# A written order for the Outlook stage: all engines, one mix a step, bands sorted by pairs of heads

## The chip, the cores and the metric

The kernel runs on one core of one Trainium2 chip. The metric is the device time of one execution in microseconds (us); of several executions the median is given. TensorE (PE) multiplies matrices, VectorE (DVE) and ScalarE (ACT) work element by element, GpSimd (POOL) and SyncE (SP) mostly issue transfers (DMAs) here. Each engine takes its own list of instructions in order and waits on semaphores of the others. Tiles lie in the on-chip memory with 128 partitions; TensorE's products land in a second small memory, PSUM.

## The reference

Two layers on an image batch of 4 x 32 x 32 positions with 384 channels. Layer 0 is an attention with group masks, followed by a mixture of four experts, two of them per token. Layer 1 is an Outlook attention, followed by a feed-forward net whose weights are Kronecker products. All is float32. The change touches the Outlook attention and its borders:

```python
v = einsum('bhwc,oc->bhwo', x, Wv)                      # x: normalised input of the layer
patches = the 3 x 3 neighbourhood of v at every position   # b, n, 9, heads, d
a = einsum('bhwc,oc->bhwo', x, Wa).reshape(b, n, 12, 9, 9)
attn = softmax(a * d ** -0.5, axis=-1)
out = einsum('bnhpq,bnqhd->bnphd', attn, patches)       # 9 outputs per position
y = sum of the 9 outputs at the positions they belong to   # a scatter-add over the 3 x 3 window
x = x + einsum('bhwc,oc->bhwo', y, Wo)
t = x + gelu(norm(x) @ kron(c_fc_1, c_fc_2).T) @ kron(c_proj_1, c_proj_2).T
```

A position gathers from its 3 x 3 window and scatters to its 3 x 3 window, so an output position depends on the values of a 5 x 5 window, with 25 coefficients per head.

## The kernel before

The 4096 tokens are 32 tiles of 128 tokens (4 rows of an image), 8 tiles an image. `attention` and `experts` come first; `rest` (L2246) then loads the residual x, the weights of Outlook, and calls `outlook` (L1764) and `Kron.run` (L2106). The Outlook stage works tile by tile:

- `scores` (L1852): normalises tile i on DVE (`xn`, L147), transposes it on PE (`ps_tr`, L155) and copies it on ACT (`xnT`, L156). PE multiplies it by Wa in two halves of 486 columns (`ps_a`, L1862); DVE takes maxima (L1871) and subtracts them (L1872), ACT takes exp (L1877), DVE sums, inverts and scales (L1879 to L1886, here called the share). Four DMAs on SyncE's queue shift the parts of the shares that belong one row up or down into the tiles `up` and `down` of this tile and its neighbours (L1898 to L1903); they copy from on-chip memory to on-chip memory. PE also makes the values `ps_v` (L1906), which ACT copies to `v` (L1910).
- `band` (L1912), two tiles later: ACT copies the outer rows of `u` (L1919, L1920), DVE adds the inner ones (L1921 to L1923), PE shifts within a row by three products (`ps_c`, L1927), DVE masks the borders (`co`, L1935). The result goes to a room in DRAM (L1942) in such a layout that reading it back with another row length (L1948) gives the band matrix of the tile: 128 source tokens by 260 target positions by 12 heads, heads innermost. Reading back waits for the writing; a band is 1560 KB.
- `gather` (L1953), three tiles after `band`: for each head PE multiplies the values (32 columns) by the band of that head (`ps_y`, L1964). Four heads go to the four groups of 32 columns of PE. The moving operand is `bands[b, t][:, j : j + hi - lo, h]`, one float out of twelve. An image is worked in two halves of 512 target positions. The last gather of a half is followed by three copies on ACT (`y`, L1973).
- `mix` (L1976): PE multiplies `y` by Wo for one tile (`ps_wo`, L1980), DVE adds the product to x (L1984). The four tiles of a half are mixed in the two steps after its last gather, two a step.

The residual of the last 15 tiles is not complete when the stage begins: `add(i)` (L1831) gathers two expert outputs per token by indirect DMAs on POOL's queue (L1540) into two buffers, adds them on DVE (L1835) and measures mean and variance (L137, L138). At the end of an image, `net.scale` takes the square root on ACT and the reciprocal on DVE (L143, L144). `loads` (L2272) issues the loads of later images at steps 1, 2 and 5 and those of Kron at step 8 (L2062 to L2080; each has a few sums on DVE, L2072 to L2077). From step 25 on `kron.begin` and `kron.shrink` (L2083, L2091) prepare the feed-forward net of the first 16 tiles: begin takes 16 pairs of statistics (L128, L129) at once.

The order of work: a step scores tile `step`, then adds, then runs what is due.

```python
at(o + 2, band, b, t)
at(o + 2 + LAG, gathered, b, 0 if t < 5 else 1, t)
...
with tc.manual_schedule(engines={eng.SP, eng.Pool}):
    outlook(net, wv, wa, wo, range(done, NT), router, kron, loads)
```

SyncE and POOL keep this written order; the order of PE, DVE and ACT in this stage is chosen by a scheduler when the program is built, which may take an instruction ahead of others and break a group of products in two. PSUM tiles for transposes, values and mixes come from one pool of two (`ps_m`).

Of the kernel before, what the change touches and what calls it, by code (L numbers as in the profile page):

```python
# [10 lines left out]
FP = mybir.dt.float32  # L11
BF = mybir.dt.bfloat16
AF = mybir.ActivationFunctionType
# [4 lines left out]
P = 128  # L18
# [1745 lines left out]
def outlook(net, wv, wa, wo, left, router, kron, loads):  # L1764
# [15 lines left out]
    with ExitStack() as ctx:  # L1780
# [5 lines left out]
        bp = ctx.enter_context(tc.tile_pool(name="ol_band", bufs=5, reuse_waits="tile"))  # L1786
# [42 lines left out]
        left = list(left)  # L1829

        def add(i):  # L1831
            for n in range(2):
                y = bp.tile([P, C], FP, name="yt", tag="yt", bufs=2)
                router.gather(y, i, n)
                nc.vector.scalar_tensor_tensor(  # L1835
                    net.x(i), y, router.weight[n][:, i : i + 1], net.x(i), ALU.mult, ALU.add
                )
            net.measure(work, i, net.x(i))

        attn, vs, bands, ys, moved = {}, {}, {}, {}, {}  # L1840
# [11 lines left out]
        def scores(b, t):  # L1852

            i = b * NB + t
            xn = work.tile([P, C], FP, name="xn", tag="xn")
            net.ln_apply(xn, i, i, net.mv, net.rs)
            xnT = work.tile([P, KC, P], FP, name="xnT", tag="xnT")
            net.transposed(ps_m, "m", xn, xnT, nc.scalar.copy)
            pa = ps_a.tile([P, 2, 512], FP, name="ps_a", tag="a")
            for hh in range(2):  # L1860
                for k in range(KC):
                    nc.tensor.matmul(  # L1862
                        pa[:, hh, :HW_], lhsT=xnT[:, k, :], rhs=wa[:, k, hh * HW_ : (hh + 1) * HW_],
                        start=k == 0, stop=k == KC - 1,
                    )

            a = ap_.tile([P, 3, 2, 3, PW], FP, name="attn", tag="attn")
            for hh in range(2):
                mx = work.tile([P, PW], FP, name="a_max", tag="a_max")
                given = pa[:, hh, :HW_].rearrange("p (q e) -> p q e", q=K2)  # L1870
                nc.vector.tensor_reduce(mx, given.rearrange("p q e -> p e q"), AX.X, ALU.max)  # L1871
                nc.vector.tensor_tensor(  # L1872
                    a[:, :, hh, :, :], given.rearrange("p (y x) e -> p y x e", y=3),
                    mx.unsqueeze(1).unsqueeze(1).to_broadcast([P, 3, 3, PW]), ALU.subtract,
                )
            flat = a.rearrange("p y s x e -> p (y s x e)")
            nc.scalar.activation(flat, flat, AF.Exp, scale=QK_SCALE)  # L1877
            rows = work.tile([P, 2, 3, PW], FP, name="a_rows", tag="a_rows", bufs=1)
            nc.vector.tensor_tensor(rows, a[:, 0], a[:, 1], ALU.add)  # L1879
            nc.vector.tensor_tensor(rows, rows, a[:, 2], ALU.add)  # L1880
            sm = work.tile([P, 2, PW], FP, name="a_sum", tag="a_sum")
            nc.vector.tensor_tensor(sm, rows[:, :, 0, :], rows[:, :, 1, :], ALU.add)
            nc.vector.tensor_tensor(sm, sm, rows[:, :, 2, :], ALU.add)
            nc.vector.reciprocal(sm, sm)
            for qi in (0, 2, 1):
                nc.vector.tensor_tensor(  # L1886
                    a[:, qi], a[:, qi], sm.unsqueeze(2).to_broadcast([P, 2, 3, PW]), ALU.mult
                )
            attn[b, t] = a


            flat = [a[:, qi].rearrange("p s x e -> p (s x e)") for qi in range(3)]
            if t == 0:
                moved[b, 0] = room(b, 0)
            if t + 1 < NB:
                moved[b, t + 1] = room(b, t + 1)
            down, up = moved[b, t]
            nc.sync.dma_start(out=up[: P - IMG, :], in_=flat[0][IMG:, :])  # L1898
            nc.sync.dma_start(out=down[IMG:, :], in_=flat[2][: P - IMG, :])
            if t:  # L1900
                nc.sync.dma_start(out=moved[b, t - 1][1][P - IMG :, :], in_=flat[0][:IMG, :])
            if t + 1 < NB:
                nc.sync.dma_start(out=moved[b, t + 1][0][:IMG, :], in_=flat[2][P - IMG :, :])  # L1903
            ps = ps_m.tile([P, 512], FP, name="ps_v", tag="m")
            for k in range(KC):
                nc.tensor.matmul(  # L1906
                    ps[:, :C], lhsT=xnT[:, k, :], rhs=wv[:, k, :], start=k == 0, stop=k == KC - 1
                )
            v = vs[b, t] = vp.tile([P, C], FP, name="v", tag="v")
            nc.scalar.copy(v, ps[:, :C])  # L1910

        def band(b, t):  # L1912


            H3 = 3 * H6
            u = work.tile([P, 6, 5, H3], FP, name="u", tag="u")
            down, up = (m.rearrange("p (g y e) -> p g y e", g=6, y=3) for m in moved.pop((b, t)))
            own = attn.pop((b, t))[:, 1].rearrange("p s x (y e) -> p (s x) y e", y=3)
            nc.scalar.copy(u[:, :, 0, :], down[:, :, 0, :])  # L1919
            nc.scalar.copy(u[:, :, 4, :], up[:, :, 2, :])  # L1920
            nc.vector.tensor_tensor(u[:, :, 1:3, :], down[:, :, 1:3, :], own[:, :, 0:2, :], ALU.add)  # L1921
            nc.vector.tensor_tensor(u[:, :, 3, :], own[:, :, 2, :], up[:, :, 1, :], ALU.add)
            nc.vector.tensor_tensor(u[:, :, 2, :], u[:, :, 2, :], up[:, :, 0, :], ALU.add)  # L1923
            pc = ps_c.tile([P, 512], FP, name="ps_c", tag="c")
# [22 lines left out]
            m = bands[b, t] = bp.tile([P, BAND, NH], FP, name="band", tag="band")  # L1947
# [5 lines left out]
        def gather(b, half, t):  # L1953

            first, last = (0, 4) if half == 0 else (3, 7)
# [3 lines left out]
            for c in range(KC):  # L1959
                if t == first:  # L1960
                    ys[c] = ps_y.tile([P, 512], FP, name=f"ps_y{c}", tag=f"y{c}")
                for n in range(4):
                    h = 4 * c + n
                    nc.tensor.matmul(  # L1964
                        ys[c][32 * n : 32 * n + 32, lo - 512 * half : hi - 512 * half],
                        lhsT=vs[b, t][:, h * HD : (h + 1) * HD],
                        rhs=bands[b, t][:, j : j + hi - lo, h],
                        start=t == first, stop=t == last, skip_group_check=True,
                    )
            if t == last:  # L1970
                y = work.tile([P, KC, 512], FP, name="y", tag="y", bufs=1)
                for c in range(KC):
                    nc.scalar.copy(y[:, c, :], ys[c])  # L1973
                return y

        def mix(b, half, n, y):  # L1976
            i = b * NB + 4 * half + n
            ps = ps_m.tile([P, 512], FP, name="ps_wo", tag="m")
            for k in range(KC):
# [3 lines left out]
                )  # L1983
            nc.vector.tensor_tensor(net.x(i), net.x(i), ps[:, :C], ALU.add)  # L1984


        later = {}

        def at(step, f, *args):
            later.setdefault(step, []).append((f, args))  # L1990

        LAG = 3
        made = {}

        def gathered(b, half, t):
            y = gather(b, half, t)
            if y is not None:
                made[b, half] = y

        def mixed(b, half, n):  # L2000
            mix(b, half, n, made[b, half])

        for b in range(B):
            for t in range(NB):
                o = b * NB + t
                at(o + 2, band, b, t)
                at(o + 2 + LAG, gathered, b, 0 if t < 5 else 1, t)
                if t == 4:
                    at(o + 2 + LAG, gathered, b, 1, 3)
                    at(o + 2 + LAG, gathered, b, 1, 4)  # L2010
            for half in range(2):
                done = b * NB + (4 if half == 0 else 7) + 2 + LAG
                for n in range(4):
                    at(done + 1 + n // 2, mixed, b, half, n)
        assert left[0] >= 2 * NB
        t_kron, first = 0, left[0]
        for step in range(B * NB + 9):
            b, t = divmod(step, NB)
            if b < B:
                scores(b, t)  # L2020
            if step == 0:
                columns()
            if step in loads:
                loads[step]()
            if step >= 4 and left:
                add(left.pop(0))

                if left and left[0] % NB == 0 or not left:
                    net.scale(first, left[0] if left else NT)
                    first = left[0] if left else NT  # L2030
            for f, args in later.pop(step, []):
                f(*args)
            if step == B * NB - 7:
                kron.begin(0)
            elif step > B * NB - 7 and t_kron < kron.GT:
# [3 lines left out]
        assert not later and t_kron == kron.GT  # L2039


class Kron:
# [39 lines left out]

    def begin(self, g):  # L2083

        self.mv, self.rs = self.net.ln_stats(range(g * self.GT, (g + 1) * self.GT), "t")
# [140 lines left out]
def metaformer_kernel(  # L2226
# [19 lines left out]
    def rest(router, done):  # L2246

        with ExitStack() as late:
# [30 lines left out]
            with tc.manual_schedule(engines={eng.SP, eng.Pool}):  # L2279
# [86 lines left out]
```

## Time and profile before

| what | us |
|---|---|
| median of 3 runs | 2829.91 (2828.95 to 2830.11) |
| the profiled execution | 2827.02 |
| its span, first to last instruction | 2825.3 |
| first score product of Outlook starts | 2269.1 |
| first product of Kron's net starts | 2737.84 |
| PE busy in the whole span | 2615.5 (93%) |
| DVE, ACT, POOL busy in the whole span | 1720.6 (61%), 1203.6 (43%), 413.8 (15%) |

The span is a little less than the time of the execution: 1.7 us lie around it. PE's clock is at full speed over most of the span, lower (0.90 to 0.93) in 20 us stretches between 2320 and 2420. DMA moves 166 GB/s in the steady part of Outlook and 236 GB/s in its busiest 20 us, 2300 to 2320. In timelines the instructions of one kind that follow each other are merged into one row: the count stands after the x, and a row's length can reach into the next row, since a product's end is modelled; the time from start to start is the one to use. A matrix product of float32 appears as two instructions.

### The profile page before, as it was taken

The numbers are of one execution on the slowest core, as the hardware profiler recorded it, in microseconds if no ns is written. First come the engines' busy times: TensorE is split into PE (matmuls) and PEld (weight loads), VectorE is DVE, ScalarE is ACT, GpSimd is POOL, SyncE is SP. The second block draws the span as 40 slices with busy tenths as digits, with TensorE's granted clock in tenths as the row PEclk, the third lists the DMA queues.
The fourth block names the chain that finished last, engine by engine and source line by source line (L and its number), as shares of the span: only waits on it lengthen the run. The fifth ranks groups of instructions, "written<-read, shape, count | busy, mean of one in ns | idle before, by whom it ended". The sixth has DMA issues, their size and how long they took to land. (4 is left out here: it accounts for less than half of the span.)

```text
span 2825.3 us, 40024 instructions
## 1 busy us (share of the span) xinstructions
PE 2615.5 (93%) x14703; PEld 1570.2 (56%) x14703; DVE 1720.6 (61%) x4382; ACT 1203.6 (43%) x2023; POOL 413.8 (15%) x501
## 2 busy tenths in 40 slices
PE   6889998999999997687999999999999988999988
PEld 3323333333333332167899999999999944444432
DVE  1377777677778787657245444655555566877742
ACT  3778777678768876312222212112112122122225
POOL 1000000030003003213211112222221101100000
PEclk9999999999999998789999999999999999999999
DMA  5143434222323242453655455565665447554432
GB/s 106 31 106 90 110 92 129 75 66 72 90 60 75 68 108 58 125 204 125 248 229 208 167 208 209 210 230 210 217 224 203 156 148 217 173 178 149 147 109 91
DMA packets 215804, 404.11 MB, mean 143 GB/s; under 512 B 83344, under 2 KB 176848, under 8 KB 202544
## 3 DMA queue, kind: packets, MB, share of 16 engines
q1 hardware_dynamic: 184496, 187.82, 22.3%
q0 software_dynamic: 26960, 209.05, 21.5%
q10 hardware_dynamic: 4144, 4.61, 0.5%
q8 instruction: 118, 1.93, 0.3%
q14 instruction: 86, 0.70, 0.1%
HBM read 304.34 MB, written 49.00 MB: 125 GB/s over the span
## 5 line engine op out<-in xcount | busy, mean ns | idle before, releaser
L1698 ACT ACTIVATE h<-ps_h,up 128x256 f32<-128x256 f32 (+1 forms) x420 | 195.1, 465 | 839.7 <-PE ps_h L1693 838.8
L1693 PE MATMUL ps_h<-xbT,up 128*128 128x256 f32 (+1 forms) x2520 | 531.8, 372 | 2.5 <-ACT h L1698 1.8
L689 DVE CUSTOM_DVE_ANT_0 e<-e,rz,inv 128x1024 f32<-128x1024 f32 x384 | 475.2, 1274 | 44.6 <-DMA rz<-r_row 44.3
L1693 PEld LDWEIGHTS ps_h<-xbT,up 128*128 128x128 f32 x2520 | 463.1, 191 | 64.5 <-ACT h L1698 2.6
L637 ACT ACTIVATE e<-ps_s,ten 128x1024 f32<-128x1024 f32 x384 | 408.1, 1110 | 64.8 <-PE ps_s L627 33.1
L627 PE MATMUL ps_s<-q,k 32*128 32x512 f32 x1536 | 295.2, 673 | 44.7 <-ACT e L637 31.4
L645 PE MATMUL ps_o<-e,wv 128*32 128x512 f32 x1536 | 226.1, 663 | 50.9 <-DVE wv L696 49.4
L1735 PE MATMUL ps_y<-wsum,hsum 128*128 128x192 f32 x1152 | 205.4, 332 | 22.8 <-DVE hsum L1656 19.6
L645 PE MATMUL ps_z<-e,rt_ones 128*32 128x512 f32 x1536 | 218.3, 642 | 0.0
L716 POOL DMA_DIRECT2D q<-po x96 | 76.1, 877 | 951.5 <-DMA q<-po 560.9
L373 ACT ACTIVATE below<-tk_left,tk_bound 128x1024 bf16<-128x1024 f32 (+1 forms) x160 | 184.4, 1152 | 52.6 <-DVE tk_bound L379 40.4
L1735 PEld LDWEIGHTS ps_y<-wsum,hsum 128*128 128x128 f32 x1152 | 190.9, 193 | 27.3 <-DVE hsum L1656 21.3
L627 PEld LDWEIGHTS ps_s<-q,k 32*128 32x128 f32 x1536 | 92.5, 193 | 182.2 <-ACT e L637 90.2
L1862 PE MATMUL ps_a<-wa,xnT 128*128 128x486 f32 x384 | 169.5, 589 | 9.2 <-DVE attn L1872 7.5
L1739 DVE TENSOR_TENSOR y<-ps_y,y 128x192 f32<-128x192 f32 x160 | 57.2, 357 | 172.0 <-PE ps_y L1735 168.8
L645 PEld LDWEIGHTS ps_o<-e,wv 128*32 128x32 f32 x1536 | 31.4, 112 | 212.5 <-DVE wv L696 64.5
L288 PE MATMUL ps_t<-xnT,wqkv 128*128 128x512 f32 x288 | 135.1, 609 | 2.4 <-ACT xnT L470 1.7
L1735 PE MATMUL ps_y<-down,h 128*128 128x192 f32 x768 | 130.0, 326 | 0.0
L1735 PEld LDWEIGHTS ps_y<-down,h 128*128 128x128 f32 x768 | 126.6, 190 | 1.9
L1862 PEld LDWEIGHTS ps_a<-wa,xnT 128*128 128x128 f32 x384 | 72.3, 194 | 95.2 <-issue 85.5
L645 PEld LDWEIGHTS ps_z<-e,rt_ones 128*32 128x32 f32 x1536 | 52.2, 117 | 131.0 <-issue 127.5
L1540 POOL DMA_INDIRECT yt<-yg,index x64 | 76.7, 1198 | 323.0 <-DVE x L1835 135.3
(392 smaller groups left out, 3539.2 us busy)
## 6 DMA issues: line engine op xcount, KB each, us to landing
band<-room SPq DMA_DIRECT2D x32, 1560.0 KB
rz<-r_row SPq DMA_DIRECT2D x48, 512.0 KB
yg<-y SPq DMA_DIRECT2D x67, 192.0 KB
q<-q SPq DMA_DIRECT2D x192, 64.0 KB
k<-k SPq DMA_DIRECT2D x192, 64.0 KB
room<-none SPq DMA_DIRECT2D x64, 192.0 KB
x<-x SPq DMA_DIRECT2D x35, 192.0 KB
o<-in_x_dram SPq DMA_DIRECT2D x33, 192.0 KB
```

The costliest lines, as they stand in the source:

```text
L288: nc.tensor.matmul(ps, lhsT=lhsT(k), rhs=rhs(k), start=k == 0, stop=k == KC - 1)
L373: nc.scalar.activation(junk[:n], left[:n], AF.Sign, bias=bound[:n], accum_out=over[:n])
L627: nc.tensor.matmul(ps[:, half * 512 : half * 512 + 512], lhsT=self.k4[r, u * P : (u + 1) * P], rhs=self.q4[r, :], start=True, stop=True,)
L637: nc.scalar.activation(e, ps, AF.Exp, bias=shift, scale=QK_SCALE)
L645: nc.tensor.matmul(ps[r : r + 32, :], lhsT=lhsT(odd), rhs=self.es[2 * u + odd][:, half * 512 : half * 512 + 512], start=u == 0, stop=u == ...
L689: nc.vector.tensor_tensor_reduce(self.es[m], self.es[m], self.rz, 1.0, self.im["inv"][:, m, self.h : self.h + 1], ALU.mult, ALU.add, self. ...
L716: nc.gpsimd.dma_start(out=there, in_=po[r : r + 32, :], accum_op=ALU.add)
L1540: self.nc.gpsimd.indirect_dma_start(out=y, out_offset=None, in_=self.net.yg[: first_row(self.complete(i // NB)), :], in_offset=bass.Indire ...
L1693: nc.tensor.matmul(ps, lhsT=up[:, o : o + P], rhs=xbT[:, k, :size], start=k == 0, stop=k == KC - 1,)
L1698: nc.scalar.activation(hs[f // 3][:, f % 3, :size], ps, AF.Gelu, bias=up[:, KC * HID + f : KC * HID + f + 1])
L1735: nc.tensor.matmul(ps, lhsT=left[f], rhs=right[:, f, :], start=f == 0, stop=f == HF - 1)
L1862: nc.tensor.matmul(pa[:, hh, :HW_], lhsT=xnT[:, k, :], rhs=wa[:, k, hh * HW_ : (hh + 1) * HW_], start=k == 0, stop=k == KC - 1,)
```

## The change

Only the Outlook stage and Kron's statistics change; every product and every DMA of before is still there. What is different:

- All five engines keep the written order in this stage (`manual_schedule` over PE, DVE, ACT, SP and POOL). The functions are cut finer, and the loop writes out a step: sort, outer, scores, exp, inner, norm of the next tile, mix, gather, transposes of the next tile, values, share, band, add, ask, gauge, Kron. LAG is now counted from the scores and is 4: the gather of tile i is in step i + 4, two steps after its band.
- `sort` is new: three ACT copies of 128 x 1040 turn a landed band (token, head) into `own` (pair of heads, token, head of the pair). The gather's moving operand is then one float out of two. `band` tiles have three buffers, `own` two, in place of five bands.
- Mixes go one a step. Where a half has only three steps for its four mixes, the last of them takes two, and the last half of all is mixed in one step of four.
- `ask` issues the two gathers of a tile at the end of a step, from step 3 on, into four buffers; `add` uses them in the next step, after the band.
- `gauge` takes Kron's first 16 statistics in the step of the mix, and `begin(0)` only the root and reciprocal.
- A step's `loads` are issued before its scores and share; before, they were after them. The DMA from a tile's first row group to its upper neighbour goes first of the four. `columns` and the first norm and transposes stand ahead of the loop.

The diff, cut to its core:

```diff
-        def add(i):
+        def ask(i):
+            y = [bp.tile([P, C], FP, name="yt", tag="yt", bufs=4) for _ in range(2)]
             for n in range(2):
-                y = bp.tile([P, C], FP, name="yt", tag="yt", bufs=2)
-                router.gather(y, i, n)
+                router.gather(y[n], i, n)
+            coming.append((i, y))
+
+        def add():
+            i, y = coming.pop(0)
+            for n in range(2):
                 nc.vector.scalar_tensor_tensor(
-                    net.x(i), y, router.weight[n][:, i : i + 1], net.x(i), ALU.mult, ALU.add
+                    net.x(i), y[n], router.weight[n][:, i : i + 1], net.x(i), ALU.mult, ALU.add
                 )
             net.measure(work, i, net.x(i))
...
+            if t:
+                nc.sync.dma_start(out=moved[b, t - 1][1][P - IMG :, :], in_=flat[0][:IMG, :])
             nc.sync.dma_start(out=up[: P - IMG, :], in_=flat[0][IMG:, :])
             nc.sync.dma_start(out=down[IMG:, :], in_=flat[2][: P - IMG, :])
-            if t:
-                nc.sync.dma_start(out=moved[b, t - 1][1][P - IMG :, :], in_=flat[0][:IMG, :])
...
-            m = bands[b, t] = bp.tile([P, BAND, NH], FP, name="band", tag="band")
+            m = landed[i] = bp.tile([P, BAND, NH], FP, name="band", tag="band", bufs=3)
...
+        def sort(i):
+            m = landed.pop(i)
+            own = bands[i] = bp.tile([P, H6, BAND, 2], FP, name="own", tag="own", bufs=2)
+            for c in range(KC):
+                pairs = slice(2 * c, 2 * c + 2)
+                nc.scalar.copy(own[:, pairs], m.rearrange("p t (n h) -> p n t h", h=2)[:, pairs])
...
-                        rhs=bands[b, t][:, j : j + hi - lo, h],
+                        rhs=bands[i][:, h // 2, j : j + hi - lo, h % 2],
...
+        LAG = 4
+        mixes = {}
         for b in range(B):
...
+            for half, steps in enumerate(((5, 6, 7, 7), (8, 9, 10, 11) if b < B - 1 else (8, 8, 8, 8))):
+                for n, step in enumerate(steps):
+                    mixes.setdefault(b * NB + step + LAG, []).append((b, half, n))
...
+        columns()
+        turn(0, norm(0))
+        for step in range(last + 1):
+            i = step
             if step in loads:
                 loads[step]()
...
+            if 0 <= i - LAG < NT:
+                sort(i - LAG)
+            if 0 <= i - 2 < NT:
+                outer(i - 2)
+            if i < NT:
+                scores(i, 0)
+                scores(i, 1)
+                exps(i)
+            if 0 <= i - 2 < NT:
+                inner(i - 2)
+            if i + 1 < NT:
+                xn = norm(i + 1)
+            done = []
+            for one in mixes.pop(step, []):
+                done.append(mix(*one))
...
+            if 0 <= i - LAG < NT:
+                gather(i - LAG, 0 if (i - LAG) % NB < 5 else 1)
+            if i + 1 < NT:
+                turn(i + 1, xn)
+            for one in done:
+                mixed(*one)
+                gauged.append(one[0])
+            if i < NT:
+                values(i)
+                share(i)
+            if 0 <= i - 2 < NT:
+                band(i - 2)
+            if 0 <= i - LAG < NT and (i - LAG) % NB == 4:
+                gather(i - LAG - 1, 1)
+                gather(i - LAG, 1)
+            if coming:
+                add()
...
+            if step >= 3 and left:
+                ask(left.pop(0))
+            while gauged and gauged[0] < kron.GT:
+                kron.gauge(0, gauged.pop(0))
+            if step == 2 * NB + LAG + 3:
                 kron.begin(0)
...
-            with tc.manual_schedule(engines={eng.SP, eng.Pool}):
+            with tc.manual_schedule(engines={eng.PE, eng.DVE, eng.Activation, eng.SP, eng.Pool}):
                 outlook(net, wv, wa, wo, range(done, NT), router, kron, loads)
```

The functions that the loop calls and that are not in the diff above hold the statements of before: `norm`, `turn`, `scores`, `exps`, `share` and `values` are the parts of the old `scores`; `outer`, `inner` and `band` those of the old `band`; `mix` and `mixed` the product and the sum of the old `mix`. `share` and `values` come in the list of SyncE and of PE as written here: loads of the step, share of tile i, room and band of tile i - 2.

## The prediction

> **What bounds the kernel now.** I read the 40 slices first, to find the stage that the change touches (Outlook: its first score product starts at 2269.1 us, the Kron stage's first `ps_h` product at 2737.84), then stretches of that stage, then TensorE's timeline. Step i below is the step that scores tile i. The stretches (columns: length, busy us of PE, weight loads, DVE, ACT, POOL; clock; DMA share; GB/s):
>
> ```profile
> core 0: us, PE busy (x) PEld busy (x) DVE busy (x) ACT busy (x) POOL busy (x), PEclk, DMA share, GB/s
> ...
> 2265.00:2735.00 470.00, 440.15 (x2027) 218.29 (x2026) 326.24 (x812) 99.83 (x195) 31.24 (x35) 0.97 0.52 168
> 2435.00:2695.00 260.00, 259.02 (x1187) 126.77 (x1189) 188.26 (x479) 57.30 (x111) 12.05 (x15) 1.00 0.51 166
> ```
>
> In the second stretch PE is busy for 259 of 260 us, DVE 188, ACT 57: the steady steps are PE's. PE's 30 idle us lie before 2435 (about 20) and after 2695. The period comes from SyncE's timeline: the first shared-attention DMA of step 3 is issued at 2310.95, of step 8 at 2382.16, of step 31 at 2698.29, which is 13.74 us a step from 8 to 31. What is in a step, from PE's timeline (start, length, instructions merged):
>
> ```profile
> 2568.67 1.99 PE L1964 MATMUL ps_y<-band,v 128*32 128x260 f32 x14
> 2570.59 0.57 PE L1927 MATMUL ps_c<-u,shift 128*128 128x180 f32 x2
> ...
> 2572.03 1.98 PE L1964 MATMUL ps_y<-band,v 128*32 128x260 f32 x10
> 2573.94 5.16 PE L1862 MATMUL ps_a<-wa,xnT 128*128 128x486 f32 x12
> 2578.93 2.10 PE L1906 MATMUL ps_v<-wv,xnT 128*128 128x384 f32 x6
> ...
> 2584.32 2.22 PE L1964 MATMUL ps_y<-band,v 128*32 128x194 f32 x24
> 2586.47 5.16 PE L1862 MATMUL ps_a<-wa,xnT 128*128 128x486 f32 x12
> ```
>
> From start to start: scores 4.99, and likewise values 1.94, one mix 1.94, band 0.92, transposes 0.42; together 10.21 us. The rest is the gather. Its 12 heads go four at a time, one to each group of 32 columns: a round. Unsplit, 194 columns take 2.15 us, 0.72 a round. The 260-column gather was split 14 + 10 by the scheduler, which makes four rounds of three: 1.92 + 1.91 us, 0.96 a round. (24 instructions of 66 with 24 of 194 take 2.94, so 66 is 0.79.) An image has four gathers of 260, four of 194, two of 66: 11.5 + 8.6 + 1.6 = 21.7 us, 2.7 a step. 10.2 + 2.7 leaves 0.8 of the 13.74: about the fourth round.
>
> What a round costs with an unbroken moving operand stands in the attention stage, four different streams to four column groups:
>
> ```profile
> 912.57 1.06 PE L645 MATMUL ps_o<-e,wv 128*32 128x512 f32 x8
> 913.45 1.04 PE L645 MATMUL ps_z<-e,rt_ones 128*32 128x512 f32 x8
> ```
>
> 0.88 us for 512 columns, 1.72 ns a column. The gather, which steps 12 floats (48 bytes) from column to column, pays 0.96/260 = 3.7 ns: 2.1 times.
>
> **The change part by part.**
>
> *Gather from pairs.* The new operand steps 2 floats (8 bytes). No row shows that step; between are 1.72 and 3.7 ns. The Trainium skill, "SBUF — State Buffer", Specifications (TRN2), says that SBUF lines are 16 bytes and that two hits in a line give full bandwidth. 48 bytes gives one hit, and the trace agrees: 3.7 ns against 1.72. 8 bytes gives two, which no row here shows. By the rule a round of 260 is 0.45 us, of 194 0.33; 66 I leave at 0.26, since issue may hold it. Image: 5.4 + 4.0 + 1.6 = 11.0, 1.4 a step, and 0.2 for the two changes of array shape (0.57 against 0.47 for the product after a gather). By the row it was measured at, 2.7 + 0.2. I take the rule: PE's step is 10.2 + 1.6 = 11.8; the other end is 13.1. The split goes in both, because the written order keeps a gather whole.
>
> *Copies on ACT.* Three copies of 1040 elements a step. Nearest rows, of other reads:
>
> ```profile
> L1877 ACT ACTIVATE attn<-attn 128x972 f32<-128x972 f32 x32 | 32.5, 1015 | 28.2 <-DVE attn L1872 28.2
> ...
> L1910 ACT COPY v<-ps_v 128x384 f32<-128x384 f32 x32 | 15.3, 480 | 141.7 <-PE ps_v L1906 134.3 <-DVE a_max L1871 7.2
> ```
>
> From them 0.91 ns an element: about 1.05 us each, 3.2 a step; 2.0 each if pairs cost double. Cover: the copies head ACT's step, and exp is not wanted before the scores and DVE's subtraction are done, at 6.3 us. 3.2 + 0.6 (the two `u` copies) is ready at 3.8, doubled at 6.8. ACT goes from 57/18.9 = 3.0 us a step to 6.3. On the path: nothing, half a us at most doubled.
>
> *One step in the written order*, by these rows. PE: scores to 5.0, mix 6.9, gather 8.4, transposes 8.9, values 10.8, band 11.8. DVE: maxima and subtractions to 6.3, inner sums 7.05, norm 7.5 (PE wants it at 8.4), mix sum 8.0, share (3.83 us in a run of the timeline) 11.8, `co` 12.4, then add 1.75 (to step 18) and gauge 0.65, ending at 14.8, 3.0 in the next step, whose maxima still end at 6.3. So PE stays the bound with some 1 us to spare. From step 24 shrinking (2 x 1.3) brings DVE to about 11.9: 0.3 us a step for 8 steps. Three table changes and the steps with two mixes: 5 us.
>
> *The wait at ACT's head.* The skill, "TensorE: Matmul & The Clock Gate" (Architectural detail), says that ACT and DVE are strict FIFO (nothing in this trace contradicts it): this speaks against the change, since the copies wait for the band's landing in front of exp and the `xnT` copy. Steady: `co` 12.4, SyncE's four share DMAs (0.63 each) end at 13.3, room lands 2.6 later, band about 6.2 later: 22.1. The copies start at 2 x 11.8 = 23.6. It holds by 1.5 us, and 2.5 more are hidden.
>
> *Kron's loads.* Their DVE sums now stand ahead of step 8's maxima; before they ran at 2409.9, 22 us after their DMAs were issued. Those DMAs are now behind a band that waits for its room:
>
> ```profile
> 2384.06 1.93 SPq L2067 DMA_DIRECT2D wf<-in_fc1T_dram  x4
> 2386.03 0.42 SPq L2068 DMA_DIRECT2D wp<-in_proj1T_dram  x1
> 2386.50 0.65 SPq L2069 DMA_DIRECT2D f<-in_fc_dram  x1
> 2387.20 0.43 SPq L2070 DMA_DIRECT2D p<-in_proj_dram  x1
> 2387.73 0.38 SPq L1942 DMA_DIRECT2D room<-co  x1
> 2391.90 0.33 SPq L1948 DMA_DIRECT2D band<-room  x1
> ```
>
> In step 7: room issued at 12, band at 16 (this one took 4.2), `f`, `p` at 20. The band's 1.56 MB and 0.96 MB of `wf`, `wp` ahead of them take about 10.5 us at 236 GB/s (the busiest 20 us), so they land near 26.5, 16 us into step 8, where DVE would have begun at 3; behind it wait norm, so PE's transposes. Loss 14 us, 1 of it for the clock, which was 0.90 to 0.93 in the stretches in which PE paused (2320 to 2420); bounds 0 (they land at once) and 20.
>
> *Other loads* now go ahead of the step's share DMAs. Steps 0 to 3 come out alike: step 3's first share DMA at 2311. Step 5's 1.5 MB delays the next step's halves by some 5 us. Steps 4 to 7 have no mix (PE 9.9); 2.4 MB a step at 236 GB/s gives 10.5.
>
> *Gathers a step ahead* free DVE of this:
>
> ```profile
> DVE x L1835 <- DMA yt<-yg,index: 20.6, 9, 5.0
> ```
>
> It is one of the reasons for PE's early idle time; its worth is in the 10.5 above and not counted again. On POOL the two issues (1.2 us each) come at the end of a step, behind the memsets of 0.36, and with four buffers wait for no sum of the same step; the slowest gather took 7.6 us to land, a step is 10. Gauging moves the 16 statistics of Kron's first half out of one batch into the steps (0.65 each, counted with DVE above); the statistics and shrinking of the second half stand, as before, in the gaps of the last steps.
>
> *The end:*
>
> ```profile
> 2718.66 0.32 SPq L1948 DMA_DIRECT2D band<-room  x1
> ...
> 2724.89 2.22 PE L1964 MATMUL ps_y<-band,v 128*32 128x194 f32 x24 [4.09 <-DMA band<-room]
> ...
> 2727.05 9.05 PE L1980 MATMUL ps_wo<-wo,y 128*128 128x384 f32 x24
> ```
>
> From step 31's share to Kron is 39.5 us. After: band 29 lands at 11, its copies end at 14 and hold up `u` of tile 31, `co` at 16; room behind band 30 to 19; band 31 lands at 25; last copy and gather 29, y 29.6, four mixes and Kron's turn 10.7: 40.3. No gain.
>
> **Sum.** Share of step 8: 2311 + 5 x 10.5 + 5 + 14 = 2382.5, as before (2382.16). To step 31: 23 x 11.8 + 2.4 + 5 = 279 against 316.1: -37. End: +1. Kron starts about 36 us earlier; its own 87 us stay. The profiled execution (2827.0 us, span 2825.3) becomes 2791, the median 2829.9 becomes 2794.
>
> **Rivals.** *Early steps better*: `f` lands soon and the loads do no harm, 14 + 5 + some 5 more: 2770. For: before, PE idles there and DVE waits for gathers; against: DMA is at 0.65 to 0.8 share there.
>
> *The pairs don't help*: 8 bytes pays like 48. PE's step 13.1, so 23 x 0.64 = 15 less 8 of stalls: 2823. For: the penalty is only shown at 48 bytes; against: the rule.
>
> *Slower: the band's landing.* With DMA denser (2.4 MB in 11.8 us is 205 GB/s against 166) room and band take longer, ACT's head waits, exp and `xnT` follow, PE and DVE stop. Room plus band is about 9 us steady and 6.9 + 6.2 = 13.1 at worst here. At 13 the copies begin 2.5 late, just hidden. A period of 14.5 needs about 18 us; that is the point. Then 23 x 0.8 = 18 more: 2848. For: 0.78 DMA share at 2300 to 2320; against: steady rooms took 2.5.
>
> **How the numbers follow.** As summed, 2780 to 2812: 0.47. Better, below 2780: 0.17. Pairs don't help, 2812 to 2832: 0.20. Slower: 0.16. About 0.2% (5.7 us) is what a measurement of this kernel can tell from no change; of the third case 0.12 is faster by more and 0.08 within. Faster 0.76, same 0.08, slower 0.16. The range 2766 to 2832 leaves out the slow case and the edge of the better one.
>
> **What would show it.** Gathers of 260 whole, about 1.4 us (2.9 means the third case); share DMAs 11.8 us apart from step 9 on; three copies of about 1.05 us; one DVE wait of about 13 us for `f` in step 8 with PE idle beside it; ACT waits for band in few steps. Wrong if copies wait for bands in every step, or if DVE's wait on PE vanishes while PE idles.

## The result: slower by 1.7%, where 1.3% faster was forecast

The median of the changed kernel is 2880.8 us (2874.5 to 2883.8, 4 runs) against 2830.0 (2829.0 to 2837.2, 4 runs) on the same chip: a ratio of 1.0169, 95% interval 1.0151 to 1.0187. The profiled execution took 2874.5 us, its span 2872.6.

The stage shows where the time went. The marks are those of the prediction: the DMA that shifts a tile's own first row group up (`up<-attn`, L1898 before, L1917 after; it was the first share DMA of a step and is now the second), and Kron's first product.

| stretch | before | after | difference |
|---|---|---|---|
| first share of step 0 to that of step 7 | 79.9 | 89.4 | +9.5 |
| step 7 to step 8 | 19.6 | 31.2 | +11.6 |
| step 8 to step 31, 23 steps | 316.1 (13.74 each) | 346.3 (15.06 each) | +30.2 |
| step 31 to Kron's first product | 39.6 | 42.1 | +2.6 |
| step 0 to Kron's first product | 455.2 | 509.1 | +53.9 |

The first share comes 5.9 us earlier, so Kron starts 48.0 us later, which is the whole difference of the two profiled executions (47.4).

The stretch from step 8 to 31 of the changed kernel, with the same columns as in the prediction:

```profile
2397.40:2743.70 346.30, 295.43 (x1461) 155.60 (x1459) 242.81 (x577) 140.72 (x208) 21.62 (x23) 0.95 0.46 149
```

PE is busy for 295 of 346 us and idle for 51, at a clock of 0.95, where the kernel before had 259 of 260 in its steady part at 1.00. No other engine is near full: DVE has 243 of 346. PE and DVE wait for each other. DVE's largest wait, then PE's waits (in all, times, longest), from 2268 to 2790:

```profile
DVE a_max L1885 <- PE ps_a L1879: 119.5, 44, 5.3
PE ps_a L1879 <- DVE attn L1886: 76.7, 32, 18.2
PE ps_tr L155 <- DVE xn L147: 20.1, 11, 2.6
PE ps_y L2002 <- ACT own L1989: 7.8, 12, 1.6
```

Once in every step a score product waits for the subtraction that reads scores. The kernel before had 7.5 us of this in the whole stage, in 4 waits. From step 8 to 31 alone, before and after:

```profile
PE ps_a L1862 <- DVE attn L1872: 0.2, 1, 0.2
PE ps_a L1879 <- DVE attn L1886: 46.3, 23, 2.7
```

PE's timeline of two steps of the changed kernel shows its place:

```profile
2549.92 2.61 PE L1879 MATMUL ps_a<-wa,xnT 128*128 128x486 f32 x6
2555.16 4.37 PE L1879 MATMUL ps_a<-wa,xnT 128*128 128x486 f32 x6 [2.64 <-DVE attn L1886]
2559.33 4.11 PE L2017 MATMUL ps_wo<-wo,y 128*128 128x384 f32 x12
2563.37 1.25 PE L2002 MATMUL ps_y<-own,v 128*32 128x194 f32 x24
...
2567.79 2.61 PE L1879 MATMUL ps_a<-wa,xnT 128*128 128x486 f32 x6
2571.85 2.71 PE L1879 MATMUL ps_a<-wa,xnT 128*128 128x486 f32 x6 [1.45 <-DVE attn L1886]
2574.40 2.10 PE L2017 MATMUL ps_wo<-wo,y 128*128 128x384 f32 x6
```

The twelve score products that stood in one row of 5.16 us before are now two rows of six, with a pause between. VectorE in the first of these steps:

```profile
2550.12 0.53 DVE L1966 TENSOR_TENSOR co<-ps_c,inside 128x150 f32<-128x150 f32 x2 [0.17 <-PE ps_c L1958]
2550.57 1.27 DVE L1841 SCALAR_TENSOR_TENSOR x<-yt,weight,x 128x384 f32<-128x384 f32 x2
...
2553.14 0.51 DVE L2141 BATCH_NORM_STATS2 ln_st<-x 128x6 f32<-128x384 f32 x1
2553.68 0.18 DVE L2142 BATCH_NORM_AGGREGATE ln_mv<-ln_st 128x2 f32<-128x6 f32 x1
2553.78 0.63 DVE L1885 TENSOR_REDUCE a_max<-ps_a 128x54 f32<-128x486 f32 x1
2554.44 0.67 DVE L1886 TENSOR_TENSOR attn<-ps_a,a_max 128x486 f32<-128x486 f32 x1
2559.57 0.66 DVE L1885 TENSOR_REDUCE a_max<-ps_a 128x54 f32<-128x486 f32 x1 [4.46 <-PE ps_a L1879]
```

PE has the first half ready at 2552.5. DVE is still at the step before (border masks, additions, statistics) until 2553.8, then takes maximum and subtraction; at 2555.2 PE starts the second half, and DVE now stands idle for 4.5 us. The two halves write different parts of `ps_a`, so the second half needs nothing of what the subtraction reads. They share one tile, though, of `[P, 2, 512]`. The section on the change says that the new functions hold the statements of before, and does not say that their order is new: `scores`, now called once for each half, has the maximum and subtraction of half 0 ahead of the products of half 1, where the old one had all twelve products first. If the program's wait follows the tile and not the bytes, this order makes the wait. That is theory A of the first experiment.

The clock adds to it. The stretches of the two steps just shown, each up to the end of the pause and then to the end of the six products (PE's granted clock is the third number from the end):

```profile
2549.90:2555.10 5.20, 2.63 (x8) 0.97 (x6) 4.49 (x12) 3.50 (x5) 0.00 (x0) 1.00 0.37 95
2555.10:2559.30 4.20, 4.14 (x6) 1.83 (x7) 0.01 (x1) 2.54 (x4) 0.00 (x0) 0.62 0.94 327
...
2567.80:2571.80 4.00, 2.60 (x8) 0.94 (x6) 3.14 (x8) 3.18 (x5) 0.00 (x0) 1.00 0.48 121
2571.80:2574.40 2.60, 2.55 (x6) 1.25 (x7) 0.00 (x0) 0.00 (x0) 0.00 (x0) 1.00 0.52 120
```

After the pause of 2.64 us the six products take 4.2 us at a clock of 0.62; after the one of 1.45 they take 2.55 at 1.00.

Step 8 has the wait that was forecast. Waits between 2366 and 2398:

```profile
PE ps_a L1879 <- DVE attn L1886: 18.2, 1, 18.2
DVE f2sum L2125 <- DMA f<-in_fc_dram: 15.5, 1, 15.5
```

### The profile page after: what moved, and what is told of

Its sections match the earlier page's. It is cut to its first block, busy times and chain, and to the rows that moved or that the text cites. A ratio compares the mean times of both kernels' runs of the same rounds, so it can differ in the third digit from the quotient of the medians.

```text
span 2872.6 us, 40227 instructions
## 1 busy us (share of the span) xinstructions
PE 2592.6 (90%) x14703; PEld 1572.8 (55%) x14703; DVE 1740.3 (61%) x4382; ACT 1299.5 (45%) x2119; POOL 416.7 (15%) x501
## 5 line engine op out<-in xcount | busy, mean ns | idle before, releaser
L1879 PE MATMUL ps_a<-wa,xnT 128*128 128x486 f32 x384 | 187.1, 628 | 77.4 <-DVE attn L1886 76.7
L373 ACT ACTIVATE below<-tk_left,tk_bound 128x1024 bf16<-128x1024 f32 (+1 forms) x160 | 184.4, 1152 | 53.9 <-DVE tk_bound L379 42.1
L1879 PEld LDWEIGHTS ps_a<-wa,xnT 128*128 128x128 f32 x384 | 73.8, 202 | 166.5 <-DVE attn L1886 101.9
```

What stands on the lines that cost most here:

```text
L373: nc.scalar.activation(junk[:n], left[:n], AF.Sign, bias=bound[:n], accum_out=over[:n])
L1879: nc.tensor.matmul(pa[:, hh, :HW_], lhsT=xnTs[i][:, k, :], rhs=wa[:, k, hh * HW_ : (hh + 1) * HW_], start=k == 0, stop=k == KC - 1,)
```

## The experiments

The sets ran on different chips, on which the kernel before took 2828 to 2874 us, so only ratios to the kernel before on the same chip are compared between sets, beside the stretches of the traces. The edits are cut to their core, some with a comment added. "Stage" is first share to Kron's first product: 455.2 before, 509.1 after.

**Two PSUM tiles** (on the changed kernel)

```diff
-pas[i] = ps_a.tile([P, 2, 512], FP, name="ps_a", tag="a")
+pas[i] = [ps_a.tile([P, 512], FP, name=f"ps_a{k}", tag=f"a{k}") for k in range(2)]
...
-pa[:, hh, :HW_], lhsT=xnTs[i][:, k, :], ...
+pa[:, :HW_], lhsT=xnTs[i][:, k, :], ...          # pa = pas[i][hh]
```

> The changed kernel, with the two halves of a step's scores in two PSUM tiles of one bank each instead of one tile of two banks; order and work unchanged. Theory A (TensorE's second half waits for VectorE's subtraction of the first half only because both lie in one tile, and so VectorE's whole backlog stands on TensorE's path): the wait of L1879 for L1886 goes from 179 us to under 30, a step of the Outlook falls from 15.06 us to 11.9 to 12.7, and the time from 2881 to about 2810 (2795 to 2830); the 15 us wait for Kron's table in step 8 remains. Rival B (VectorE has more work in a step than before and is itself the bound, the wait is only where it shows): 2865 to 2885, with the idle time moved to another instruction of TensorE.

Ratio 0.989 [0.986, 0.992]; stage 422.6; 12.04 us a step from 8 to 31, most steps 11.7. On the 2830 of the first chip that is 2799. (The 179 us of the expectation adds up two views of the same pauses: 76.7 us before PE's products and 101.9 before its weight loads.) PE's waits from 2427 to 2705, and the stretch:

```profile
PE ps_tr L155 <- DVE xn L147: 4.2, 2, 2.1
PE ps_y L2002 <- ACT own L1989: 0.8, 1, 0.8
```
```profile
2427.60:2704.40 276.80, 272.26 (x1467) 150.59 (x1465) 242.01 (x577) 142.23 (x209) 21.60 (x23) 1.00 0.57 186
```

The score wait is gone. Nothing else was changed, so theory A is shown and rival B falls: DVE does the same 242 us of work in 277 us as it did in 346 in the changed kernel. In these two executions the tile cost 69.5 us in the 23 steps, in two parts that can be read off the two stretches: 50.9 - 4.5 = 46.4 us of idle PE, and 295.4 - 272.3 = 23.1 us of products at a lower clock.

**Both halves' products first, one tile**

```diff
                 scores(i, 0)        # the products alone
                 scores(i, 1)
+                level(i, 0)         # maximum and subtraction
+                level(i, 1)
```

> The changed kernel, one tile as it is, but with the products of both halves written ahead of the two maxima and subtractions, as the kernel before has them. Theory A: the wait inside a step goes as well, VectorE's first maximum starts 2.5 us later in the step, which its spare time takes: 2800 to 2840, within 15 us of the version with two tiles. Rival B: 2865 to 2885.

Ratio 0.999 [0.998, 1.001]; stage 459.2; 12.87 a step, most steps 12.2. On the 2830 of the first chip that is 2828: inside theory A's 2800 to 2840, but 29 us from the two tiles, where at most 15 were expected. The wait inside the scores is gone too, and yet over a third of the gain is missing (the ratio fell by 0.018, with two tiles by 0.028). A step of its timeline:

```profile
2559.22 5.05 PE L1879 MATMUL ps_a<-wa,xnT 128*128 128x486 f32 x12
...
2564.11 2.10 PE L2019 MATMUL ps_wo<-wo,y 128*128 128x384 f32 x6
...
2564.31 0.66 DVE L1887 TENSOR_REDUCE a_max<-ps_a 128x54 f32<-128x486 f32 x1 [1.25 <-PE ps_a L1879]
...
2567.51 0.47 DVE L147 TENSOR_SCALAR xn<-x,mv_x,rs_x 128x384 f32<-128x384 f32 x1
...
2568.04 0.55 PE L155 MATMUL ps_tr<-ident,xn 128*128 128x128 f32 x3 [0.31 <-DVE xn L147]
```

DVE's largest wait from step 8 to 31:

```profile
DVE a_max L1887 <- PE ps_a L1879: 41.6, 23, 4.1
```

With one tile the first maximum waits for the second half's products. DVE stands idle for that (1.25 us here, 1.8 a step in the mean), and with its 10.5 us of work a step (240.8 in 23) that makes 12.3. PE comes to its transposes before the norm is there (19 waits, 13.7 us). I had taken DVE's spare time to be enough. Under the written order the tile costs whichever way the halves are written, and only its division lets DVE start at half time.

**Kron's sums late** (on the changed kernel)

```diff
         8: lambda: kron.load(fc1T, fc2, proj1T, proj2),
+        12: lambda: kron.sums(),    # f2sum, row, wide
```

> The changed kernel, with the three VectorE instructions on Kron's tables (the sum of f, the rows of the identity, their product with p) written in step 12 instead of step 8, its loads left in step 8. If the step from share 7 to share 8 takes 31 us because VectorE stands at the sum of f until that table lands: 12 to 18 us less, 2863 to 2869. If the landing of the other tables or the loads on SP's queue set that step: within 3 us of 2881.

Ratio 1.009 [1.006, 1.012] where the changed kernel has 1.017; step 7 to 8 takes 13.2 in place of 31.2, which is 18.0. Step 8 did what was expected, at the upper end; the ratio moved by 0.0081, 23 us, more than that. The rest came from steps 8 to 31, 338.6 us for 346.3:

```profile
2418.20:2756.80 338.60, 286.84 (x1465) 152.62 (x1463) 242.95 (x578) 141.20 (x209) 21.63 (x23) 0.97 0.47 153
```

PE is idle as long as in the changed kernel (51.8 us, 50.9 there); what is less is its busy time (286.8 for 295.4), at a clock of 0.97 for 0.95. The last section comes back to this.

**Pairs alone, on the kernel before**

```diff
+def sort(b, t): ...                # three copies on ACT, bands of 3, own of 2
-rhs=bands[b, t][:, j : j + hi - lo, h],
+rhs=owns[b, t][:, h // 2, j : j + hi - lo, h % 2],
+at(o + 1 + LAG, sort, b, t)
```

> The kernel before, with only the copies of the band into pairs by ScalarE, one step ahead of the gather, and the gather from them (the ring of bands 3 and 2 sorted ones in place of 5); everything else is left to the scheduler. If the gather is on TensorE's path at what its columns cost, 8-byte steps instead of 48-byte steps save some 1.2 us in each of 32 steps: 2790 to 2800. If the scheduler's order or the copies on ScalarE take that back: 2825 to 2840.

Ratio 0.996 [0.994, 0.997], or 2818 on the first chip's 2830: a gain, a third of what the first expectation had, and more than the second. From step 8 to 31 PE's busy time fell from 310.1 to 288.0 us, but the stretch only from 316.1 to 307.9: idle time grew from 6 to 20 us, and the clock fell from 0.99 to 0.96. PE's named waits there are many and small (for a mix's sum 6.5 us, for `attn`, `xnT`, `a_rows`, `own` 1.6 to 3 each). Which of the scheduler's choices makes them is open.

**Two tiles and late sums**: both edits together.

> The version with two PSUM tiles, and the three VectorE instructions on Kron's tables written in step 12. If the two waits are independent: step 8 falls from 26.0 us to about 12.5, steps stay at 11.7, first share to Kron 422.6 - 13.5 = 409, and the ratio to the kernel before goes from 0.989 to about 0.984. If step 8 of that version is held by something else (the landing of x of the last image, SP's queue): 0.987 to 0.990.

Ratio 0.9815 [0.980, 0.983], 2774.2 us beside 2827.7, a little better than the 0.984 expected. Stage 408.4, step 7 to 8 12.6, 11.93 a step. This version beats both kernels. One step of PE:

```profile
2541.53 2.10 PE L2017 MATMUL ps_wo<-wo,y 128*128 128x384 f32 x6
2543.55 1.24 PE L2002 MATMUL ps_y<-own,v 128*32 128x194 f32 x24
2544.72 0.55 PE L155 MATMUL ps_tr<-ident,xn 128*128 128x128 f32 x3
2545.11 2.10 PE L1926 MATMUL ps_v<-wv,xnT 128*128 128x384 f32 x6
...
2547.96 5.05 PE L1879 MATMUL ps_a<-wa,xnT 128*128 128x486 f32 x12
```

Twelve score products in one row again, and no pause behind them.

**How the band is laid out** (on that version; three kernels): no copies and 48-byte steps; copies by fours of heads, 16-byte steps; a plane for each head, 4-byte steps.

```diff
-rhs=bands[i][:, h // 2, j : j + hi - lo, h % 2],
+rhs=bands[i][:, j : j + hi - lo, h],             # no copies
+rhs=bands[i][:, h // 4, j : j + hi - lo, h % 4], # fours
+rhs=bands[i][:, h, j : j + hi - lo],             # planes
```

> As the version with two tiles and late sums, but ScalarE copies nothing and the gather reads the landed band at 48-byte steps, in the same order. If TensorE is now the bound of a step, the gather's three rounds of 260 columns cost 3 x 0.96 = 2.9 us in place of 1.5: steps of 13.1 in place of 11.7, 1.4 x 32 = 44 us more, ratio 0.999 or so. If VectorE or the landing of the bands bounds the step by now, the steps stay within 0.3 us of 11.7 and the ratio at 0.984 to 0.988.

> The same version with heads in fours: the copies move 16 contiguous bytes for every place, and the gather reads every fourth float (16-byte steps, one element in each 16-byte line) in place of every second. If what counts is two elements to a line, a round of 260 costs 0.8 to 0.96 us, near the 0.96 of 48-byte steps: ratio 0.995 to 1.000. If a step of four floats is as good as a step of two: rounds of 0.5 us, ratio 0.984 as with pairs.

> The same version with a plane for every head: the gather reads contiguous columns, the copies gather single floats at 48-byte steps. If a round is then as the contiguous products of the heads before (1.72 ns a column, 0.45 us for 260 columns): a step 0.15 us shorter than with pairs, 5 us in all, ratio 0.982. If the copies of single floats take longer than the 1.12 us of the pairs (over 2 us each), ScalarE's exponentials come late and it is slower than the pairs: 0.988 or more.

Ratios 0.990 [0.988, 0.992], 0.990 [0.987, 0.993] and 0.988 [0.986, 0.990], beside 0.9815 with pairs; 13.06, 13.22 and 12.15 us a step beside 11.93. The gather of 260 columns (busy us in 23 steps, mean ns of one of 24 products), in the order pairs, no copies, fours, planes:

```profile
L2002 PE MATMUL ps_y<-own,v 128*32 128x260 f32 x288 | 19.1, 396 | 0.0
```
```profile
L1999 PE MATMUL ps_y<-band,v 128*32 128x260 f32 x288 | 34.8, 629 | 0.0
```
```profile
L2001 PE MATMUL ps_y<-own,v 128*32 128x260 f32 x288 | 35.4, 637 | 0.0
```
```profile
L1989 ACT COPY own<-band 128x1040 f32<-128x1040 f32 x70 | 139.1, 2056 | 15.3 <-DMA band<-room 15.3
L2002 PE MATMUL ps_y<-own,v 128*32 128x260 f32 x288 | 18.8, 388 | 1.3 <-ACT own L1989 1.3
```

Each row holds 12 gathers: 1.59, 2.90, 2.95 and 1.57 us apiece. So 8 bytes is nearly as good as 4, and 16 as bad as 48. The step follows: 13.06 - 11.93 = 1.13 us for a mean of 1.2 us of gather, which shows that PE is the bound here. The ratios of the first two kernels, 0.990, still lie below the expected 0.999 and 0.995 to 1.000: I had counted 1.4 us in all 32 steps, and without copies it is 1.13 in the last 23, with 4.0 us won back ahead of step 7. Planes lose elsewhere: copying single floats takes ScalarE 2.06 us in place of 1.12, and the end grows from 39.8 to 47.4 us, where PE waits for `own` 13.8 us in place of 7.6.

**Rows asked for in the step that adds them** (on the same version)

```diff
+            if step >= 4 and left:
+                ask(left.pop(0))
             if coming:
                 add()
...
-            if step >= 3 and left:
-                ask(left.pop(0))
```

> The fastest version so far (two tiles, late sums), with each tile's two gathers of expert rows asked in the same step as, and straight ahead of, the two additions that read them, where the changed kernel asks a step ahead. VectorE then stands at its additions until the rows land. If asking ahead is worth what VectorE waited for these rows in the kernel before (9 waits, 20.6 us, longest 5.0) or more, since the order of VectorE is now fixed and the landing of a gather is a few us: some 2 to 5 us in each of the steps that add, 20 to 50 us more, ratio 0.989 to 0.999. If VectorE's spare time in a step takes the wait: within 5 us, 0.980 to 0.984.

Ratio 0.981 [0.979, 0.983], 11.93 a step, stage 402.8: the place of the asking is worth nothing that these runs can tell, and DVE still has no wait for rows. GpSimd's long waits are for buffers (`yt` until the additions 107 us, `up` 191), so it runs ahead of the step as far as its buffers let it. I then took two of the four `yt` buffers away:

```diff
-y = [bp.tile([P, C], FP, name="yt", tag="yt", bufs=4) for _ in range(2)]
+y = [bp.tile([P, C], FP, name="yt", tag="yt", bufs=2) for _ in range(2)]
```

> The version that asks for its expert rows in the step that adds them, with two buffers for these rows (one step's) instead of four. If what takes VectorE's wait away is that GpSimd's queue runs ahead of the step as far as the buffers reach, and not the place where the asking is written: with two buffers a gather can only start when the additions of the step before have read them, so VectorE's waits for rows stay near zero only if a step (11.7 us) is longer than the landing of two gathers (7.6 us for the slowest before); then within 5 us, ratio 0.979 to 0.983. If the landing is longer than that, VectorE waits 1 to 5 us in each adding step, 10 to 40 us more, ratio 0.985 to 0.995.

Ratio 0.983 [0.980, 0.986], stage 407.0, no wait for rows: the two intervals overlap. What is left to explain the end of DVE's 20.6 us of waiting is the place of the additions at the end of the step in DVE's own list, a step behind the additions that freed the buffers. This is argued, not shown: no run changed that place by itself.

**Two tiles on the kernel before**

```diff
-pa = ps_a.tile([P, 2, 512], FP, name="ps_a", tag="a")
+pas = [ps_a.tile([P, 512], FP, name=f"ps_a{k}", tag=f"a{k}") for k in range(2)]
```

> The kernel before, with only the two halves of the scores in two PSUM tiles; scheduler as it is. If the single tile costs only where a product is written behind a reading of the other half (the changed kernel), the kernel before, which writes both products first, has nothing to gain: within 0.3% of 1.000 (TensorE's whole wait for the subtraction is 7.5 us there). If two tiles are worth something in themselves, by an earlier maximum: 0.985 to 0.995.

Ratio 0.999 [0.998, 1.001]. The tile costs nothing under the old order; it is the written order with the one tile that costs.

## Why the prediction was wrong

**The step that failed** is "One step in the written order", in its words "PE: scores to 5.0" and "whose maxima still end at 6.3. So PE stays the bound with some 1 us to spare". It laid PE's and DVE's lists side by side and let them meet only where data passes. The program makes them meet once more, at the tile. PE's second half waits until DVE, whose tail of the step before reached 3.9 us into this one (3.0 in the sum), has subtracted the first half; scores end at 6.6 in the second step shown and at 9.4 in the first, not at 5.0, and DVE's second maximum waits in turn. In the first step shown that is 2.64 us of pause and 1.6 of lower clock. The run with two tiles gives the sum's own figures back: steps of 11.7 (11.8 forecast), 276.8 us from step 8 to 31 (279), a ratio that makes 2799 of 2830 (2794). Neither sign of being wrong that the prediction named appeared: copies did not wait for bands in every step, and DVE's wait for score products did not vanish but grew, from 39.9 us to 119.5. The Trainium skill, "PSUM — Partial Sum Buffer" (PSUM bank collisions raise a hardware error), keeps two engines apart on one bank and partition quadrant, and says that different banks run clean. The halves are 512 floats apart, in two banks, so by that rule the wait isn't the chip's; the run with two tiles agrees.

**Gather from pairs**: right in mechanism and size. From start to start a gather of 260 columns takes 1.52 us and one of 194 takes 1.17. With three rounds each that is 1.74 ns a column (1.72 forecast) and some 0.16 us that does not grow with the columns, where the sum had 0.2 for the changes of shape. Contiguous columns took 1.45 and 1.13. The rule on 16-byte SBUF lines held at its edge: 16-byte steps, one hit a line, took 2.95 us where 8-byte ones took 1.59.

**"The other end is 13.1"**: the run without copies has 13.06. The rival "pairs don't help" is refuted; its step was right.

**Copies on ACT**: 1.12 us each for 1.05, hidden in the steady steps. Not at the end: PE's 7.8 us of waits for `own` all lie behind 2740.

**The wait at ACT's head**: it holds. ACT waited for a band in 4 of 32 steps, 17.6 us in all, so the slower rival was right in its sign and wrong in its mechanism; it would have shown as waits of `own`, not of `ps_a`.

**Kron's loads**: 15.5 us of waiting for `f` against about 13, a loss of 18.0 (sums late against after) or 13.4 (the same with two tiles) against 14. Right.

**Other loads, early steps**: steps 4 to 7 took 13.15 each (12.72 with late sums) against 10.5. With two tiles it is 11.65, with late sums too 12.10, and without copies (two tiles, late sums) 11.05. So 0.6 to 1.5 us of the miss is the tile's and 0.6 to 1.0 goes with the copies, which wait for the first bands (9.2 us in the version with late sums). For the last half us the runs show no cause: 10.5 was too low. The share of step 3 came at 2313.5 (2311 forecast).

**Gathers a step ahead**: counted at nothing of its own, and worth nothing of its own.

**The end**: 42.1 against 40.3, 39.8 with two tiles.

The stage of the changed kernel can now be built from the runs: before 455.2; written order with two tiles, late sums and no copies 428.6, so -26.6; pairs -20.2 (408.4); sums back in step 8 +14.2 (422.6); one tile for both halves +86.5 (509.1). Each figure is of one profiled execution, and with late sums the tile costs 74.2 (408.4 to 482.6). The ratios, from several executions each, agree better: the tile costs 0.028 with the sums in step 8 (0.989 to 1.017) and 0.027 with late sums (0.9815 to 1.009), 77 to 79 us of 2830.

The failure could have been read ahead of the run. The old trace has the score products in one unbroken row of twelve, with the maxima behind them; the change writes a reading of the tile between its two writings. I looked at what each instruction reads, and not at which tile the program would wait for.

## What to carry to other kernels

When you write out an order for several engines by hand, list for each tile who writes and who reads it in the new order: where a write followed another engine's read of the same tile, there was a wait here, though they touched different parts. Give parts that different engines use in turn tiles of their own. And it paid here to let TensorE find two of the floats that it streams in each 16 bytes (steps of 8 bytes): contiguous floats brought only 0.07 us more in a gather of 1.52, and cost ScalarE twice the time to make, where the pairs were made behind TensorE's work.

## What was not expected of the hardware

A pause of TensorE costs twice, but not always. Of the 25 pauses of 1 us or more between 2400 and 2740 in the changed kernel, none of the 8 of 1.45 us was followed by a lower clock; of the 17 of 2.1 to 2.7 us, 11 were. The clock behind one of 2.63 us, in stretches of 2 us:

```profile
2431.99:2433.99 2.00, 2.00 (x4) 1.01 (x5) 0.00 (x0) 1.98 (x4) 0.00 (x0) 0.80 0.80 159
2433.99:2435.99 2.00, 2.00 (x4) 0.80 (x3) 0.00 (x0) 0.50 (x1) 0.00 (x0) 0.50 0.74 281
2435.99:2437.99 2.00, 2.00 (x7) 1.17 (x6) 1.85 (x5) 0.49 (x1) 0.00 (x0) 0.85 0.94 399
```

That is 0.4 + 1.0 + 0.3 = 1.7 us lost, as at half speed for 3.4; the other ten lost the same within 0.02. 11 x 1.7 = 19 of the 23.1 us of slower products. In the run with Kron's sums late the pauses are nearly the same, 8 of 1.45 us and 17 of 2.1 us or more, but only 5 of the 17 were followed by a lower clock, which accounts for its shorter steps. Length alone does not decide it: a pause of 2.65 us at 2704 had no lower clock behind it, one of 2.08 at 2493 had. Where a second pause of 2.1 us came within 6 us of another, the clock fell behind it in all four cases of the two runs. What else decides is open. The Trainium skill, "TensorE: Matmul & The Clock Gate" (HAM oscillation — how this bites in real kernels), gives idle gaps over some 3.4 us as the ones to avoid; here gaps of 2.1 to 2.7 us were enough in 11 cases of 17 in one run and in 4 of 16 in the other, and the measurement decides.
